# A diffusion transformer block on one core: bias products moved ahead of unit 0, their weights on the scalar queue, weight casts on GpSimd, and two units' statistics one beat later

## The chip, the cores and the metric

The kernel runs on 1 core of one Trainium2 chip. The metric is the device time of one execution in microseconds (us). The engines are TensorE (PE, matrix products; its weight loads are listed as PEld), VectorE (DVE), ScalarE (ACT), GpSimd (POOL) and SyncE (SP). SP issues most of the DMA transfers, ACT and POOL a few.

## The reference

A transformer block with adaptive layer norm, for 16 batch entries of 256 tokens with 256 channels, 16 heads of 16 channels, all in float32:

```python
shift_a, scale_a, gate_a, shift_m, scale_m, gate_m = split(silu(c) @ W_mod + b_mod, 6)
x_norm = ln(x) * (1 + scale_a) + shift_a
q, k, v = split(x_norm @ W_qkv + b_qkv, 3)
x = x + gate_a * (softmax(q k^T * hd**-0.5) v @ W_proj + b_proj)     # self attention
q_c = ln(x) @ W_qc + b_qc;  k_c, v_c = split(ln(context) @ W_kvc + b_kvc, 2)
x = x + (softmax(q_c k_c^T * hd**-0.5) v_c @ W_cproj + b_cproj)      # cross attention
x_norm2 = ln(x) * (1 + scale_m) + shift_m
x = x + gate_m * (gelu(x_norm2 @ W_mlp1 + b_mlp1) @ W_mlp2 + b_mlp2)
```

The biases of the values need not be added to the values: since attention weights sum to one, they can be carried through the projection. The kernel computes `gate_a`, `(bias_v @ W_proj + b_proj) * gate_a` and `bias_vc @ W_cproj + b_cproj` once, each as a narrow matrix product, and adds them later.

## The kernel before, in words

**Units and beats.** There are 32 attention units, numbered n = 0 to 31: self attention (`s`) of batch entries 0 to 3, then alternately self attention of entry b + 4 and cross attention (`c`) of entry b. The main loop runs `beat(n, k)` for n = -1 to 31 and k = 0 to 7. In beat (n, k), PE computes a first set of scores of unit n + 1 (tile `s`), whose row maxima VectorE takes (`mx`), and transposed scores of unit n (tile `st`), which ScalarE exponentiates (`pt`). In "unit -1", the slot ahead of unit 0, only the first scores of unit 0 are there. Between the scores stand the other units' pieces: layer norm statistics (`st_`, `mv_`, `rs_`, on VectorE), their power and application (`rs_`, `xn_`, on GpSimd), transposes (`psT_`), query, key and value products (`ps_q`, `ps_k`, `ps_v`, in "lanes" of two interleaved halves), the weighted sums (`o`), and the projection (`ps_P`). The scores use two PSUM banks, which the next scores may overwrite once `mx` has read them.

**High and low parts.** Products are made with a rounded high part and a low part of each operand (`h_`/`l_`, `xTh`/`xTl`, `W[0]`/`W[1]`). `split` makes the two parts of a weight: a copy that rounds, and a subtraction on GpSimd. Queries and keys are written to a stack (`big`) by DMA (`send`), with rows of ones (`one0`, `one1`, `one2`, for three buffers) and of negated maxima (`m`).

**Order.** Each engine keeps the program order of the code (`keep_in_program_order`). What stands outside the beats is placed by two tables of words: `PRE` is the order ahead of the loop, and `SL` says which words run at the end of which beat. `rest` takes one further step of the generator `setup_rest`. `cN` and `dN` are N products of zeros (`wz`), into a bank that is not in use. `ld2`, `ld3`, `ld4` load x of units 2, 3, 4. `HP` chooses the engine of the copy in `split`: 0 is VectorE, 1 is GpSimd; its first entry is for the weights of `setup_rest`.

**setup_rest before.** In ten steps: load `wga`, `wp` and the bias rows; load `wkc`, `wqc`; `ps_ga` and its sum into `gb`; `ps_pb`, two sums into `gb`, and the store `gd<-gb`; load `wvc`, `wcp`; split Wp, Wkc, Wqc, Wvc; `ps_cb`, its sum `bc`, the store `cd<-bc`, and the split of Wcp. All its DMAs are on SP. `gb` has a buffer of the tag `pt`, of which there are five.

**Statistics of self units.** In beat (n, 4) the statistics of unit n + 4 (`ls`) follow, on VectorE, those of the cross unit n + 3 (`lx`), where that unit's are taken in this beat (`late`: batch entries 0, 1, 14, 15). With a self unit at n + 4, this happens at n = 2 and n = 4.

Of the kernel before, what the change touches and what calls it, by code (L numbers as in the profile page):

```python
# [13 lines left out]
ALU = mybir.AluOpType  # L14
AX = mybir.AxisListType

P = 128
# [4 lines left out]
def pixart_block(  # L22
# [8 lines left out]
    B, N, H = x.shape  # L31
# [4 lines left out]
    KC = H // P  # L36
# [15 lines left out]
                return tc.keep_in_program_order(i) if self.on else i  # L52
            return issue

    E_ = {'M': ((-17, -12, -10, -1, 1), (0, 3, 4, 7, 9), (8, 11, 13, 15)), 'CUT': 8, 'LN': {'s': 'pool', 'c': 'pool', 'q': 'pool'}, 'ON': (1, 1, 1), 'L0': -16, 'L1': 1, 'S0': -7, 'A0': 0, 'T0': 1, 'H': (7, 11, 14, 15), 'S1': 5, 'A1': 7, 'L2': 9, 'T1': 9, 'S2': 32, 'AP': 23, 'DV': (0, 1), 'HP': (0, 0), 'BZ': {}, 'AV': {1: [(1, 2), (1, 3)], 9: [(0, 0), (0, 1)]}, 'AHEAD': (0, 0, 0, 0, 0, 2), 'W1P': [(-9, 1), (-8, 1), (-7, 1), (-6, 1), (-5, 1), (-5, 5), (-4, 1), (-4, 3), (-4, 5), (-3, 1), (-3, 3), (-3, 5), (-2, 1)], 'W2P': [(-4, 7), (-3, 0), (-3, 4), (-3, 6), (-3, 7), (-2, 2), (-2, 4), (-2, 6), (-1, 0), (-1, 1)], 'XP': 1, 'IL': 1, 'MF': 0, 'SH': 4, 'RAMP': 1, 'HA': 1, 'MP': 16, 'W': (7, 1, 0, 0), 'PRE': 'z0qp z0kp load silu b12 brow L0a turn L0b b4 L0d scale T0t sc1 hik lok T0h T0l b4 shift b4 hiq L1a L1b bk loq K0a K0b K0x0 K0x1 K0y0p K0y1p L1d T1t K0l T1h K0l0 K0l1 Q0a Q0m bq Q0h Q0x0 Q0y0p Q0x1 Q0y1p T1l Q0l Q0l0 Q0l1 z1kp z1qp K1a K1b hiv lov Q1a Q1b K1x0 K1x1 K1y0 K1y1 K1l K1l0 K1l1 ld2 Q1x0 Q1x1 Q1y0 Q1y1 Q1l Q1l0 Q1l1 V0a V0b bv b5 one0 vone ld3 z2kp z2qp', 'SL': {(-1, 0): 'one1 one2 c4', (-1, 1): 'ld4 L2a V1a', (-1, 2): 'L2b L2c V1b', (-1, 3): 'c5', (-1,4): 'M0 c4', (-1, 5): 'T2t T2h T2l c3', (-1, 6): 'rest L3a K2a c1', (-1, 7): 'K2m L3b L3p L3c c3', (0, 0): 'rest d4', (0, 1): 'rest', (0, 2): 'd3', (0, 3): 'rest', (0, 4): 'rest', (0, 5): 'rest', (0, 6): 'rest', (1, 1): 'rest', (1, 3): 'rest', (1, 5): 'rest', (30, 0): 'd3', (30, 1): 'd2', (30, 2): 'd3', (30, 5): 'd3', (31, 1): 'd2'}}

    PE = InOrder(nc.tensor, True)
    ACT, DVE, POOL, SP = (InOrder(e, True) for e in (nc.scalar, nc.vector, nc.gpsimd, nc.sync))
# [9 lines left out]
    def ps_gen(name, tag=None):  # L68


        if tag is None and ps_turn[0] is not None:
            ps_turn[0] ^= 1
            tag = (SHORT, LONG)[ps_turn[0]]
        tag = tag or SHORT
        return psum.tile([P, 512], F32, tag=tag, name=name, bufs=2)
# [16 lines left out]
    BMOD, BQKV, BQC, BKVC, BM1 = 0, 12, 18, 20, 24  # L92
# [11 lines left out]

    brow = const.tile([32, P], F32, name="brow")

    def stage(w_ap, c0, name, tag="pt", bufs=5, t=None):

        if t is None:
            t = work.tile([P, KC, H], F32, tag=tag, name=name, bufs=bufs)  # L110
        SP.dma_start(t, w_ap[:, c0:c0 + H].rearrange("(k p) c -> p k c", p=P))
        return t

    def split(hi, lo, src, eng=POOL, hp=0):
# [11 lines left out]
    sc1 = const.tile([P, 2, 2, B], F32, name="sc1")  # L126
    bT = const.tile([P, 32], F32, name="bT")
# [3 lines left out]
    cd = dram.tile([1, H], F32, name="cd", bufs=1)  # L131
# [89 lines left out]
    def setup_rest():  # L221
        gb = work.tile([B, 2, 2, H], F32, tag="pt", name="gb", bufs=5)
        gA, bb = gb[:, 0], gb[:, 1]
        bc = const.tile([1, H], F32, name="bc")
        wg, wp = stage(W_mod, 2 * H, "wga", "g", 3), stage(W_proj, 0, "wp_f", "g", 3)
        SP.dma_start(bb[:, 0], b_mod[2 * H:3 * H].partition_broadcast(B))
        SP.dma_start(bb[:, 1], b_proj.partition_broadcast(B))
        SP.dma_start(bc, b_cproj.partition_broadcast(1))
        yield
        wkc, wqc = stage(W_kvc, 0, "wkc_f", "g", 3), stage(W_qc, 0, "wqc_f", "c", 2)  # L230
        yield
        pst = ps_gen("ps_ga")
        for k in range(KC):
            PE.matmul(pst[:B, :H], sT[:, k], wg[:, k], start=(k == 0), stop=(k == KC - 1))
        DVE.tensor_tensor(gA[:, 0], pst[:B, :H], bb[:, 0], ALU.add)
        yield
        pst = ps_gen("ps_pb")
        for k in range(KC):
            PE.matmul(pst[:B, :H], bqkv[:, 4 + k], wp[:, k], start=(k == 0), stop=(k == KC - 1))
        DVE.tensor_tensor(gA[:, 1], pst[:B, :H], bb[:, 1], ALU.add)  # L240
        DVE.tensor_tensor(gA[:, 1], gA[:, 1], gA[:, 0], ALU.mult)
        SP.dma_start(gd[:, 0:2], gA)
        yield
        wvc, wcp = stage(W_kvc, H, "wvc_f", "x1", 5), stage(W_cproj, 0, "wcp_f", "x1", 5)
        yield
        split(Wp[0], Wp[1], wp)
        yield
        split(Wkc[0], Wkc[1], wkc)
        yield
        split(Wqc[0], Wqc[1], wqc)  # L250
        yield
        split(Wvc[0], Wvc[1], wvc)
        yield
        pst = ps_gen("ps_cb")
        for k in range(KC):
            PE.matmul(pst[:1, :H], bT[:, BKVC + 2 + k:BKVC + 3 + k], wcp[:, k],
                      start=(k == 0), stop=(k == KC - 1))
        DVE.tensor_tensor(bc, pst[:1, :H], bc, ALU.add)
        SP.dma_start(cd, bc)
        split(Wcp[0], Wcp[1], wcp)  # L260


# [423 lines left out]
    M = {}  # L686
# [256 lines left out]
    def beat(n, k):  # L943
# [29 lines left out]
        if k == 0:  # L973
            if cur:
                m_part(cur, 1)
            exps()
            if prev:
                av_part(prev, 2)
                av_part(prev, 3)
            if q2:  # L980
                q2.K.low()
                q2.K.send_low()
            if p3:
                p3.add()
            if ls and n > 0:
                load(ls)
            if lc:
                lc.ln[0].steps[0]()
            if p1:
                p1.gate()  # L990
        elif k == 1:
            exps()
            run(lanes(q2 and q2.Q, p2))
            if lc:
                lc.ln[0].steps[1]()
                lc.ln[0].steps[2]()
        elif k == 2:
            exps()
            if prev:
                p1.turn(1)  # L1000
            if q3T:
                q3T.T[0].turn()
                q3T.T[0].high()
            if p2 and p2.hurry:
                p2.add()
        elif k == 3:
            exps()
            if q3T and q3T.kind == "s":
                q3T.T[0].low()
            if prev:  # L1010
                p1.norm(1)
            run(lanes(q2 and q2.V, q2 and q2.Q))
            if q3T and q3T.kind == "c":
                q3T.T[0].low()
        elif k == 4:
            if nxt:
                m_part(nxt, 0)
            exps()
            if cur:
                av_part(cur, 0)  # L1020
                av_part(cur, 1)
            if prev:
                p1.aT.turn()
                p1.aT.high()
            if q2:
                q2.Q.low()
                q2.Q.send_low()
            if p3:
                p3.store()
            if late:  # L1030
                for f in lx.ln[1].steps:
                    f()
            if ls:
                ls.ln[0].steps[0]()
                ls.ln[0].steps[1](False)
        elif k == 5:
            exps()
            run(lanes(q3 and q3.K, q2 and q2.V))
            if prev:
                p1.aT.low()  # L1040
            if ls:
                ls.ln[0].pow()
                ls.ln[0].steps[2]()
            if early:
                early.ln[1].steps[0]()
            v = unit(n + 5)
            if v and v.kind == "c":
                load(v)
        elif k == 6:
            exps()  # L1050
            if cur:
                cur.post.begin()
                cur.post.turn(0)
            if lx:
                lx.T[1].turn()
                lx.T[1].high()
            if early:
                early.ln[1].steps[1]()
                early.ln[1].steps[2]()
            if prev and whole:  # L1060
                p1.proj(0)
                p1.proj(1)
        elif k == 7:
            exps()
            run(lanes(None if whole else p1, q3 and q3.K))
            if prev and whole:
                p1.end()
                p1.add()
                p1.store()
            if cur:  # L1070
                cur.post.norm(0)
            if lx:
                lx.T[1].low()
# [97 lines left out]
```

## Time and profile before

| | |
|---|---|
| Time, 3 runs | 819.60, 819.81, 820.62 us; median 819.81 |
| Profiled execution | 822.69 us, of which span 820.9 us |
| PE, PEld, DVE, ACT, POOL busy | 786.1, 662.8, 600.0, 584.6, 461.8 us |
| TensorE clock granted, mean | 0.997 of full speed |
| Costliest on VectorE: `mx` | 256 x 1223 ns |
| Costliest on ScalarE: `pt` | 256 x 1019 ns |
| HBM read, written | 26.97 MB, 8.46 MB |
| Chain that ended last | PE 66%, DVE 18%, issue 4%, POOL 3%, DMA 3% |

The span runs from the first to the last instruction; the time of an execution is longer by what lies around it. Busy time is the time in which an engine had an instruction under way. A row of a timeline gives the start in us, the duration in us, the engine, the line, the operation, output and inputs by the program's names, the shapes and types, how many instructions were merged, and in brackets the idle time before it and what ended it. Nearly all instructions carry the line of the recording helper (L51), so they are told apart by their tiles. "SPq" marks an issue by the queue of SP.

### The profile page before, as it was taken

To read this page: it belongs to the slowest core of one execution; us is meant where nothing else is said; L and a number is where in the kernel's file an instruction comes from. 1 tells how busy PE (TensorE), PEld (TensorE's weight loads), DVE (VectorE), ACT (ScalarE), POOL (GpSimd) and SP (SyncE) were. 2 spreads that over 40 slices of the span, in tenths; PEclk is the share of its full clock that TensorE was granted. 3 is DMA by queue.
4 is the path that set the end of the run, shared out by engine and by line. 5 is a ranking of instruction groups with operands and counts; after the bars stand their busy time and mean duration, and the time that the engine had idled before them with its cause. 6 is when DMAs were issued, how large, how long until landed. Compare 5 with 4: busy or idle time off the path is not lost.

```text
span 820.9 us, 23768 instructions
## 1 busy us (share of the span) xinstructions
PE 786.1 (96%) x9485; PEld 662.8 (81%) x9485; DVE 600.0 (73%) x1055; ACT 584.6 (71%) x1022; POOL 461.8 (56%) x399
## 2 busy tenths in 40 slices
PE   8899999999999999999999999999889999999997
PEld 8777777777787777778777778877658999999997
DVE  4787878888887888887787888777664566566562
ACT  3266878788887877878788888887556666665663
POOL 5544647464754636475463767654445656566663
PEclk9999999999999999999999999999999999999999
DMA  5553434344453444435344554534311212212211
GB/s 146 169 146 104 130 106 131 96 128 110 113 157 91 132 112 124 123 106 151 96 137 109 153 141 130 151 98 122 102 54 41 74 57 77 72 46 78 78 37 55
DMA packets 89938, 87.88 MB, mean 107 GB/s; under 512 B 9506, under 2 KB 85572, under 8 KB 89828
## 3 DMA queue, kind: packets, MB, share of 16 engines
q1 hardware_dynamic: 89364, 85.58, 37.0%
q8 instruction: 75, 1.23, 0.6%
q0 software_dynamic: 192, 0.52, 0.2%
q14 instruction: 35, 0.29, 0.1%
q10 hardware_dynamic: 272, 0.26, 0.1%
HBM read 26.97 MB, written 8.46 MB: 43 GB/s over the span
## 4 chain that ended last, share of the span: by engine, by line
PE 66%; DVE 18%; issue 4%; POOL 3%; DMA 3%; SPq 1%; ACT 1%; POOLq 0%; ACTq 0%
PE s L51 14%; DVE mx L51 12%; PE o L51 12%; PE ph L51 11%; PE st L51 9%; PE ps_q L51 3%; PE ps_kc L51 2%; PE ps_P_s L51 2%; PE ps_qc L51 2%; PE ps_k L51 2%; DMA c<-in_ctx_dram 2%; PE ps_v_s L51 1%; DVE xTl_s L51 1%; PE psT_m L51 1%; PE psm L51 1%
## 5 line engine op out<-in xcount | busy, mean ns | idle before, releaser
L51 DVE TENSOR_REDUCE mx<-s 128x4 f32<-128x1024 f32 x256 | 313.1, 1223 | 103.1 <-PE s L51 98.4
L51 ACT ACTIVATE pt<-st 128x1024 f32<-128x1024 f32 x256 | 260.9, 1019 | 54.6 <-PE st L51 45.4
L51 PE MATMUL s<-big 63*128 63x256 f32 x1024 | 121.2, 310 | 17.9 <-DVE mx L51 15.8
L51 PE MATMUL o<-pt,v 128*32 128x256 f32 x2048 | 123.8, 382 | 3.1 <-DVE A_s L51 3.1
L51 PEld LDWEIGHTS s<-big 63*128 63x128 f32 x1024 | 80.1, 186 | 55.4 <-DVE mx L51 34.3
L51 POOL TENSOR_TENSOR hl<-hf,hh 128x512 fp32r<-128x512 f32 x64 | 89.0, 1399 | 55.5 <-ACT hh L51 54.5
L51 PE MATMUL st<-big 64*128 64x256 f32 x1024 | 107.2, 282 | 2.3 <-ACT pt L51 2.3
L51 PEld LDWEIGHTS o<-pt,v 128*32 128x32 f32 x2048 | 60.0, 109 | 44.9 <-DVE A_s L51 5.7
L51 PEld LDWEIGHTS st<-big 64*128 64x128 f32 x1024 | 82.0, 188 | 4.4 <-ACT pt L51 2.9
L51 ACT ACTIVATE hf<-ph,bT 128x256 f32<-128x256 f32 x120 | 50.3, 473 | 28.1 <-PE ph L51 28.1
L51 ACT COPY oT<-o 128x512 f32<-128x512 f32 x63 | 36.9, 586 | 45.7 <-PE o L51 45.7
L51 ACT ACTIVATE hh<-ph,bT 128x256 fp32r<-128x256 f32 x120 | 50.4, 471 | 24.8 <-PE s L51 13.0
L51 POOL TENSOR_TENSOR xTl_as<-y_as,xTh_as 128x512 fp32r<-128x512 f32 x16 | 20.3, 1270 | 64.9 <-ACT y_as L51 64.9
L51 POOL TENSOR_TENSOR xTl_c<-y_c,xTh_c 128x512 fp32r<-128x512 f32 x16 | 20.6, 1290 | 61.7 <-PE s L51 52.9
L51 PE MATMUL ph<-wqch,wself 128*128 128x256 f32 x256 | 51.8, 285 | 0.0
L51 PE MATMUL ph<-wkch,wself 128*128 128x256 f32 x256 | 51.8, 286 | 0.0
L51 POOL TENSOR_TENSOR xTl_ac<-y_ac,xTh_ac 128x512 fp32r<-128x512 f32 x16 | 20.5, 1280 | 51.7 <-ACT y_ac L51 47.8
L51 PE MATMUL s<-big,hh 128*128 128x256 f32 x256 | 47.4, 282 | 0.0
L51 PE MATMUL st<-big,hh 128*128 128x256 f32 x256 | 47.2, 281 | 0.0
L51 DVE TENSOR_SCALAR xn_m<-x,mv_m,rs_m 128x256 f32<-128x256 f32 x32 | 38.3, 1236 | 10.8 <-POOL rs_m L51 10.8
L51 PEld LDWEIGHTS ph<-wqch,wself 128*128 128x128 f32 x256 | 42.0, 191 | 0.4 <-issue 0.4
L51 PEld LDWEIGHTS ph<-wkch,wself 128*128 128x128 f32 x256 | 41.9, 191 | 0.4
(221 smaller groups left out, 2381.9 us busy)
## 6 DMA issues: line engine op xcount, KB each, us to landing
big<-h_kc SPq DMA_DIRECT2D x64, 128.0 KB
big<-h_qc SPq DMA_DIRECT2D x64, 128.0 KB
big<-h_k SPq DMA_DIRECT2D x62, 128.0 KB
big<-h_q SPq DMA_DIRECT2D x62, 128.0 KB
big<-l_k SPq DMA_DIRECT2D x32, 128.0 KB
big<-l_q SPq DMA_DIRECT2D x32, 128.0 KB
c<-in_ctx_dram SPq DMA_DIRECT2D x16, 256.0 KB
g<-gd SPq DMA_DIRECT2D x16, 256.0 KB
```

The source lines that it names most:

```text
L51: i = f(*a, **k)
```

## The change

The three bias products (`ps_ga`, `ps_pb`, `ps_cb`) move to the beats 3, 4 and 5 of unit -1, where they stand in place of products of zeros (`c5`, `c4`, `c3`). Their weights (`wga`, `wp`, `wcp`) and bias rows are loaded together, by DMAs that the scalar queue issues, in the last part of `PRE`. The loads of `wkc`, `wqc` and `wvc` become one step, at the end of unit -1. The five splits follow in beats (0, 1), (0, 4), (1, 0), (1, 2), (1, 4), and their copies are on GpSimd. `ld2` moves ahead of the sends of unit 1; `one0`, `one1` and `one2` move from the end of `PRE` and beat (-1, 0) to the beats (-1, 0), (-1, 3) and (-1, 7). In the beats with `late`, all statistics of `ls` move from beat 4 to beat 5, behind that beat's `mx`.

```diff
-    E_ = {... 'HP': (0, 0), ...
+    E_ = {... 'HP': (1, 0), ...
 'PRE':
-  ... Q0l1 z1kp z1qp K1a ... K1l1 ld2 Q1x0 ... V0a V0b bv b5 one0 vone ld3 z2kp z2qp
+  ... Q0l1 ld2 z1kp z1qp K1a ... K1l1 Q1x0 ... V0a V0b bv b5 rest vone ld3 z2kp z2qp
 'SL':
-  (-1, 0): 'one1 one2 c4', (-1, 3): 'c5', (-1, 4): 'M0 c4', (-1, 5): 'T2t T2h T2l c3',
-  (-1, 6): 'rest L3a K2a c1', (-1, 7): 'K2m L3b L3p L3c c3', (0, 0): 'rest d4', (0, 1): 'rest',
-  (0, 2): 'd3', (0, 3): 'rest', (0, 4): 'rest', (0, 5): 'rest', (0, 6): 'rest',
-  (1, 1): 'rest', (1, 3): 'rest', (1, 5): 'rest'
+  (-1, 0): 'one0 c4', (-1, 3): 'rest one1', (-1, 4): 'M0 rest', (-1, 5): 'T2t T2h T2l rest',
+  (-1, 6): 'L3a K2a c1', (-1, 7): 'K2m L3b L3p L3c c3 one2 rest', (0, 0): 'd4', (0, 1): 'rest',
+  (0, 2): 'd3', (0, 4): 'rest', (1, 0): 'rest', (1, 2): 'rest', (1, 4): 'rest'
...
-    def stage(w_ap, c0, name, tag="pt", bufs=5, t=None):
+    def stage(w_ap, c0, name, tag="pt", bufs=5, t=None, q=SP):
...
-        SP.dma_start(t, w_ap[:, c0:c0 + H].rearrange("(k p) c -> p k c", p=P))
+        q.dma_start(t, w_ap[:, c0:c0 + H].rearrange("(k p) c -> p k c", p=P))
...
-        wg, wp = stage(W_mod, 2 * H, "wga", "g", 3), stage(W_proj, 0, "wp_f", "g", 3)
-        SP.dma_start(bb[:, 0], b_mod[2 * H:3 * H].partition_broadcast(B))
-        SP.dma_start(bb[:, 1], b_proj.partition_broadcast(B))
-        SP.dma_start(bc, b_cproj.partition_broadcast(1))
-        yield
-        wkc, wqc = stage(W_kvc, 0, "wkc_f", "g", 3), stage(W_qc, 0, "wqc_f", "c", 2)
+        wg, wp = stage(W_mod, 2 * H, "wga", "g", 3, q=ACT), stage(W_proj, 0, "wp_f", "g", 3, q=ACT)
+        ACT.dma_start(bb[:, 0], b_mod[2 * H:3 * H].partition_broadcast(B))
+        ACT.dma_start(bb[:, 1], b_proj.partition_broadcast(B))
+        ACT.dma_start(bc, b_cproj.partition_broadcast(1))
+        wcp = stage(W_cproj, 0, "wcp_f", "x1", 5, q=ACT)
...
-        wvc, wcp = stage(W_kvc, H, "wvc_f", "x1", 5), stage(W_cproj, 0, "wcp_f", "x1", 5)
...
         SP.dma_start(cd, bc)
+        yield
+        wkc, wqc = stage(W_kvc, 0, "wkc_f", "g", 3), stage(W_qc, 0, "wqc_f", "c", 2)
+        wvc = stage(W_kvc, H, "wvc_f", "x1", 5)
+        yield
+        split(Wp[0], Wp[1], wp)
...
-            if ls:
+            if ls and not late:
                 ls.ln[0].steps[0]()
                 ls.ln[0].steps[1](False)
         elif k == 5:
...
-            if ls:
+            if ls and late:
+                for f in ls.ln[0].steps:
+                    f()
+            elif ls:
                 ls.ln[0].pow()
                 ls.ln[0].steps[2]()
```

More of the change, by code (lines that the diff above doesn't have):

```diff
@@ L53, in __getattr__ @@
             return issue
-    E_ = {'M': ((-17, -12, -10, -1, 1), (0, 3, 4, 7, 9), (8, 11, 13, 15)), 'CUT': 8, 'LN': {'s': 'pool', 'c': 'pool', 'q': 'pool'}, 'ON': (1, 1, 1), 'L0': -16, 'L1': 1, 'S0': -7, 'A0': 0, 'T0': 1, 'H': (7, 11, 14, 15), 'S1': 5, 'A1': 7, 'L2': 9, 'T1': 9, 'S2': 32, 'AP': 23, 'DV': (0, 1), 'HP': (0, 0), 'BZ': {}, 'AV': {1: [(1, 2), (1, 3)], 9: [(0, 0), (0, 1)]}, 'AHEAD': (0, 0, 0, 0, 0, 2), 'W1P': [(-9, 1), (-8, 1), (-7, 1), (-6, 1), (-5, 1), (-5, 5), (-4, 1), (-4, 3), (-4, 5), (-3, 1), (-3, 3), (-3, 5), (-2, 1)], 'W2P': [(-4, 7), (-3, 0), (-3, 4), (-3, 6), (-3, 7), (-2, 2), (-2, 4), (-2, 6), (-1, 0), (-1, 1)], 'XP': 1, 'IL': 1, 'MF': 0, 'SH': 4, 'RAMP': 1, 'HA': 1, 'MP': 16, 'W': (7, 1, 0, 0), 'PRE': 'z0qp z0kp load silu b12 brow L0a turn L0b b4 L0d scale T0t sc1 hik lok T0h T0l b4 shift b4 hiq L1a L1b bk loq K0a K0b K0x0 K0x1 K0y0p K0y1p L1d T1t K0l T1h K0l0 K0l1 Q0a Q0m bq Q0h Q0x0 Q0y0p Q0x1 Q0y1p T1l Q0l Q0l0 Q0l1 z1kp z1qp K1a K1b hiv lov Q1a Q1b K1x0 K1x1 K1y0 K1y1 K1l K1l0 K1l1 ld2 Q1x0 Q1x1 Q1y0 Q1y1 Q1l Q1l0 Q1l1 V0a V0b bv b5 one0 vone ld3 z2kp z2qp', 'SL': {(-1, 0): 'one1 one2 c4', (-1, 1): 'ld4 L2a V1a', (-1, 2): 'L2b L2c V1b', (-1, 3): 'c5', (-1,4): 'M0 c4', (-1, 5): 'T2t T2h T2l c3', (-1, 6): 'rest L3a K2a c1', (-1, 7): 'K2m L3b L3p L3c c3', (0, 0): 'rest d4', (0, 1): 'rest', (0, 2): 'd3', (0, 3): 'rest', (0, 4): 'rest', (0, 5): 'rest', (0, 6): 'rest', (1, 1): 'rest', (1, 3): 'rest', (1, 5): 'rest', (30, 0): 'd3', (30, 1): 'd2', (30, 2): 'd3', (30, 5): 'd3', (31, 1): 'd2'}}
@@ new lines, in pixart_block @@
+    E_ = {'M': ((-17, -12, -10, -1, 1), (0, 3, 4, 7, 9), (8, 11, 13, 15)), 'CUT': 8, 'LN': {'s': 'pool', 'c': 'pool', 'q': 'pool'}, 'ON': (1, 1, 1), 'L0': -16, 'L1': 1, 'S0': -7, 'A0': 0, 'T0': 1, 'H': (7, 11, 14, 15), 'S1': 5, 'A1': 7, 'L2': 9, 'T1': 9, 'S2': 32, 'AP': 23, 'DV': (0, 1), 'HP': (1, 0), 'BZ': {}, 'AV': {1: [(1, 2), (1, 3)], 9: [(0, 0), (0, 1)]}, 'AHEAD': (0, 0, 0, 0, 0, 2), 'W1P': [(-9, 1), (-8, 1), (-7, 1), (-6, 1), (-5, 1), (-5, 5), (-4, 1), (-4, 3), (-4, 5), (-3, 1), (-3, 3), (-3, 5), (-2, 1)], 'W2P': [(-4, 7), (-3, 0), (-3, 4), (-3, 6), (-3, 7), (-2, 2), (-2, 4), (-2, 6), (-1, 0), (-1, 1)], 'XP': 1, 'IL': 1, 'MF': 0, 'SH': 4, 'RAMP': 1, 'HA': 1, 'MP': 16, 'W': (7, 1, 0, 0), 'PRE': 'z0qp z0kp load silu b12 brow L0a turn L0b b4 L0d scale T0t sc1 hik lok T0h T0l b4 shift b4 hiq L1a L1b bk loq K0a K0b K0x0 K0x1 K0y0p K0y1p L1d T1t K0l T1h K0l0 K0l1 Q0a Q0m bq Q0h Q0x0 Q0y0p Q0x1 Q0y1p T1l Q0l Q0l0 Q0l1 ld2 z1kp z1qp K1a K1b hiv lov Q1a Q1b K1x0 K1x1 K1y0 K1y1 K1l K1l0 K1l1 Q1x0 Q1x1 Q1y0 Q1y1 Q1l Q1l0 Q1l1 V0a V0b bv b5 rest vone ld3 z2kp z2qp', 'SL': {(-1, 0): 'one0 c4', (-1, 1): 'ld4 L2a V1a', (-1, 2): 'L2b L2c V1b', (-1, 3): 'rest one1', (-1,4): 'M0 rest', (-1, 5): 'T2t T2h T2l rest', (-1, 6): 'L3a K2a c1', (-1, 7): 'K2m L3b L3p L3c c3 one2 rest', (0, 0): 'd4', (0, 1): 'rest', (0, 2): 'd3', (0, 4): 'rest', (1, 0): 'rest', (1, 2): 'rest', (1, 4): 'rest', (30, 0): 'd3', (30, 1): 'd2', (30, 2): 'd3', (30, 5): 'd3', (31, 1): 'd2'}}
@@ L243, in setup_rest @@
         yield
-        wvc, wcp = stage(W_kvc, H, "wvc_f", "x1", 5), stage(W_cproj, 0, "wcp_f", "x1", 5)
+        pst = ps_gen("ps_cb")
+        for k in range(KC):
+            PE.matmul(pst[:1, :H], bT[:, BKVC + 2 + k:BKVC + 3 + k], wcp[:, k],
+                      start=(k == 0), stop=(k == KC - 1))
+        DVE.tensor_tensor(bc, pst[:1, :H], bc, ALU.add)
+        SP.dma_start(cd, bc)
+        yield
+        wkc, wqc = stage(W_kvc, 0, "wkc_f", "g", 3), stage(W_qc, 0, "wqc_f", "c", 2)
+        wvc = stage(W_kvc, H, "wvc_f", "x1", 5)
         yield
@@ L253, in setup_rest @@
         yield
[L254 to L259, printed above, removed]
         split(Wcp[0], Wcp[1], wcp)
```

## The prediction

> **What bounds the kernel now.** I read the busy shares first, then stretches by unit, then VectorE row by row from 25 to 82 us, where the edits lie, and last the granted clock.
>
> ```profile
> span 820.9 us, 23768 instructions
> PE 786.1 (96%) x9485; PEld 662.8 (81%) x9485; DVE 600.0 (73%) x1055; ACT 584.6 (71%) x1022; POOL 461.8 (56%) x399
> ```
>
> TensorE is nearly always busy and VectorE's `mx` is next: a beat is scores (`s`), then their row maximum (`mx`), which frees the banks for the next scores. From `mx` to `mx` a beat with no extras takes 1.82 us. The stretches run from the first `mx` of one unit's beats to the next: units -1, 0, 1, 2, 3.
>
> ```profile
> 25.66:40.85 15.19, 13.43 (x105) 10.90 (x105) 12.44 (x20) 2.53 (x6) 5.46 (x6) 1.00 0.51 152
> 40.85:60.22 19.37, 18.37 (x204) 14.21 (x200) 15.41 (x27) 11.48 (x17) 8.51 (x8) 1.00 0.49 135
> 60.22:81.88 21.66, 19.78 (x237) 15.16 (x234) 15.57 (x27) 13.53 (x22) 10.36 (x10) 0.92 0.41 115
> 81.88:99.90 18.02, 17.52 (x250) 14.03 (x246) 14.53 (x26) 14.94 (x25) 11.08 (x10) 1.00 0.48 133
> 99.90:117.72 17.82, 16.97 (x246) 13.55 (x242) 14.22 (x24) 14.01 (x23) 10.56 (x10) 1.00 0.38 107
> ```
>
> Columns: stretch, length, busy us of PE, weight loads, VectorE, ScalarE, GpSimd, granted clock, DMA. Unit 1 does less than unit 3, yet is 3.84 us longer and alone has a clock below 1. Its VectorE rows, and unit 0's, name the causes:
>
> ```profile
> 48.99 0.87 DVE L51 SCALAR_TENSOR_TENSOR xTl_s<-psT_s,sc,xTh_s 128x256 fp32r<-128x256 f32 x2
> 50.48 0.41 DVE L51 TENSOR_TENSOR gb<-ps_pb,gb 16x256 f32<-16x256 f32 x1 [0.62 <-PE ps_pb L51]
> 50.92 0.41 DVE L51 TENSOR_TENSOR gb<-gb 16x256 f32<-16x256 f32 x1
> 51.27 1.21 DVE L51 TENSOR_REDUCE mx<-s 128x4 f32<-128x1024 f32 x1
> ...
> 61.36 0.87 DVE L51 SCALAR_TENSOR_TENSOR l_k<-ps_k,bqkv,h_k 128x256 fp32r<-128x256 f32 x2
> 63.50 0.75 DVE L51 BATCH_NORM_STATS2 st_c<-c 128x6 f32<-128x256 f32 x2 [1.27 <-DMA c<-in_ctx_dram]
> 64.17 1.21 DVE L51 TENSOR_REDUCE mx<-s 128x4 f32<-128x1024 f32 x1
> ```
>
> `mx` stands behind the bias sums, and behind statistics of a context tile that lands late. After that wait the clock halves:
>
> ```profile
> 62.07:65.48 3.41, 2.56 (x30) 2.00 (x22) 2.14 (x6) 1.61 (x2) 1.08 (x1) 1.00 0.65 190
> 65.48:68.89 3.41, 3.41 (x22) 2.85 (x24) 1.76 (x4) 1.54 (x3) 3.16 (x4) 0.53 0.29 78
> ```
>
> **The change, part by part.** Terms are shifts of the `mx` chain, in the time of the profiled execution (822.69 us, span 820.9). It is 2.88 above the median 819.81; I take the same saving off both.
>
> *Unit -1, added: +0.4.* `ps_ga` (0.97 on PE) takes the place of five zero products (1.38), `ps_pb` of four (1.06), `ps_cb` of three (0.83). PE still ends each before `mx` frees the banks, save `ps_cb`: 34.68 + 0.58 of transposes + 0.97 = 36.2, under VectorE's 36.24. On VectorE, which idles 0.60 ahead of `mx`, the first `gb` sum (0.41) hides. The next two (0.79 to the next `mx`) delay one `mx` by 0.2, absorbed because `xTl` waits for ScalarE's `xTh` until 36.21 anyway. `bc` (0.41) follows `xTl` directly and is paid. Bounds: 0.34 (overlap of VectorE rows) to 1.64 (all four exposed).
>
> *Unit 0, removed.* `ps_ga` at 44.41 stands between the lanes and the next scores, whose banks were free at 44.0: -0.97. `ps_pb` and two sums: scores could end at 49.9 and `xTl` ends at 49.86, so `mx` at 51.27 moves to 49.95: -1.32. Next, `pt` waits 1.38 for `gd<-gb` to free its buffer, holding PE's `st` 0.51. With that gone, PE reaches the scores of beat 6 at 53.3 on this scale and `mx` stands at 53.8 where it was 56.34, 2.55 earlier: -0.26 more. The casts of `wself` and `wkch` (0.42) lie before `mx` rows that wait for PE by 0.55 and 0.27: nothing.
>
> *Unit 1, removed.* `c` is issued at 58.45, behind two weight loads and a queue that had stood at `gd`, and lands 5.03 later. In the new order the sends follow at once and the loads are out of its way: sync issues it near 54.8, `st_c` is due near 60.0, so 5.2 suffice; unit 3's `st_c` at 101.83, of a `c` issued at 96.67, waits for nothing. -1.2. With no wait PE idles at most 0.3, and I take the half clock as gone: beat 2 to 3 took 3.06 against 1.82 in unit 3: -1.24 (bounds 0 to -1.71, half of 3.41). `wqch` hides; `wvch` delays `mx` by 0.33, but the `o` products wait for `A_s` as before: nothing net. `ps_cb`, `bc` and `wcph` make beat 5 to 6 3.35 long against 1.92: -1.43. Check: 21.66 - 3.87 = 17.79, beside unit 3's 17.82.
>
> *GpSimd's five copies: nothing, if short.* The trace has no GpSimd copy. Bounds: 0.54 (memset of 128x512) to 2.44 (two 128x256 scalar operations); I take 1.28, the subtraction of the same shape. Three copies and three subtractions (7.7) stand ahead of `xTl_as`, with `xg`, `rs_c` and `xn_c` (1.3 + 0.8 + 2.4). Starting when `g` lands, 58.7 to 61.1, they end by 70.7 to 73.4; with `xTl_as`, 72.0 to 74.7. PE needs it at 80.96 - 5.9 = 75.05.
>
> The Trainium skill speaks against this move: "GPSIMD Engine Reference", Engine selection, says not to put elementwise work there, two-input operations being about twice as slow, one-input roughly at line rate. The trace agrees on the first: VectorE casts in 0.42, GpSimd subtracts in 1.28. By the page's 1.03 cycles an element a copy would be about 0.44 plus dispatch (an estimate), and the sum unchanged.
>
> *Self statistics (units 2 and 4): -0.2.* Three kinds of rows (1.0 to 1.1 in all) leave the space before `mx` at 94.36, whose scores were done at 93.55: `mx` 0.76 earlier. They then stand before the next one: 0.41 earlier. Then PE's `psT_q` waits for `xn_q`, which GpSimd ends at 96.68 either way: 0.1 remains, twice. Bounds 0 to -1.5.
>
> *Queues.* The scalar queue stands idle from 23.81 to 30.22; six issues of 0.28 to 0.61 fit. But the new order lets `bc` wait for `wga` and `wcp` for `wp` to land, and ScalarE's `v` copy (due 30.22, used by `psm` at 32.85) stands behind them; sync's third `h_q` send waits for `gb`. `ld2` fills a wait of sync's. `one0`, `one1`, `one2` pass x loads and are needed from 40.7 on. `wkc`, `wqc`, `wvc` now stand before unit 2's `h_k` sends: 0.8 late, needed a unit later; `m` follows them to about 45.2, due at 49.2.
>
> **Sum:** +0.4 - 0.97 - 1.32 - 0.26 - 1.2 - 1.24 - 1.43 - 0.2 = -6.2. Profiled 816.5, median 813.6. Later units repeat their own beats, so the lead is kept.
>
> **The rivals.**
>
> *Slow GpSimd copies.* At 2.44 each, three add 3.5 to a margin of 0.3 to 3.0: PE stands 0.5 to 3.2 at `xTl_as`; the middle, 1.8, gives 815.4. For: two-scalar operations take 1.22 for half the elements. Against: a copy reads one operand less than the 1.28 row.
>
> *The half clock stays, or comes into unit -1*, where narrow products (16 columns, 1 column) take over from full zeros: 814.8 for one stretch, 816.5 if a new one costs 1.7 on top. For: it came in a window where PE was busy 2.56 of 3.41. Against: 27.93 to 31.35 had 2.60 and stayed full. The skill's "TensorE: Matmul & The Clock Gate", on the idle window, says half rate follows at least one idle window of about 3.4 us. The trace's stretch is 3.41 long, as it says, but PE had idled only 0.85 before it, so the row decides; by the page alone, removing that wait need not bring the clock back, and the sum would be -5.0.
>
> *The scalar queue lands late: slower.* PE stands in order at `ps_cb`, due 35.3. At the slowest landing in these rows (5.03), `wp`, issued at 24.4, lands at 29.4, and `wcp` after it at 34.5 to 35.0: just in time. Each microsecond beyond is paid in full; from `wcp` at 41.5 the gain is gone. At 10 us a landing it comes at 44.4: 9.1 lost, 2.9 slower, 822.7. For: q1 sends share the engines, busy 0.79 from 24.5 to 27.9. Against: 0.60 and 0.34 after that.
>
> **How the numbers follow.** Forecast 0.62; copies 0.12; clock 0.14; late landings 0.12, of which 0.08 beyond the whole gain and 0.04 near it. A measurement of this kernel tells about 0.2% (1.6 us) from no change, so faster 0.88, same 0.04, slower 0.08. The range goes down by the rest of the statistics' bound (1.3) and part of the +0.4 to 812.0, and up to 817.2 over the copies and both clock cases; the late landings stay out.
>
> **What would show it.** Right: stretches near 15.6, 16.8 and 17.8 for units -1, 0 and 1; `st_c` and `pt` without DMA waits; clock 1.00 throughout; GpSimd copies under 1.5. Wrong: PE waiting for `wga`, `wp` or `wcp`; a half-clock stretch; `xTl_as` ending after its lane begins. The forecast falls if units 0 and 1 together save under 4 us.

## The result, and the profile after

The changed kernel takes 815.53 us (median of 6 runs, 815.27 to 815.80) against 819.75 us for the kernel before in the same comparison (6 runs, 819.09 to 824.08): a ratio of 0.994, 95% interval 0.9919 to 0.9960. It is faster, by 0.6%, and the time lies inside the forecast's range (812.0 to 817.2), but the saving of the medians is 4.2 us where 6.2 was forecast. The two profiled executions differ by more, 822.69 to 815.38, which is 7.3. Most of the study is about these two distances from 6.2.

The page of the changed kernel, and its stretches by unit (-1 to 3) with the columns of the stretches shown before:

```profile
span 813.6 us, 23717 instructions
PE 780.9 (96%) x9461; PEld 658.9 (81%) x9461; DVE 597.9 (73%) x1050; ACT 585.2 (72%) x1022; POOL 464.6 (57%) x404
```

```profile
25.55:41.07 15.52, 13.23 (x93) 8.90 (x93) 13.76 (x25) 2.53 (x6) 5.47 (x6) 1.00 0.61 167
41.07:57.35 16.28, 15.78 (x196) 13.43 (x192) 13.50 (x21) 11.38 (x17) 9.64 (x10) 1.00 0.54 157
57.35:75.24 17.89, 16.93 (x234) 13.52 (x230) 14.61 (x23) 13.45 (x22) 11.47 (x12) 1.00 0.43 116
75.24:93.04 17.80, 17.40 (x250) 13.96 (x246) 14.68 (x27) 14.93 (x25) 10.93 (x10) 1.00 0.46 128
93.04:111.03 17.99, 17.12 (x246) 13.73 (x242) 14.21 (x23) 14.17 (x24) 10.93 (x10) 1.00 0.39 108
```

Units -1, 0 and 1 take 15.52, 16.28 and 17.89 (forecast 15.6, 16.8, 17.8) where they took 15.19, 19.37 and 21.66, together 6.53 less. Unit 1 costs no more than its neighbours, and the clock is 1.00 in every stretch.

VectorE's rows of the changed kernel show the sums in unit -1, and unit 1 without its wait:

```profile
34.03 0.41 DVE L51 TENSOR_TENSOR gb<-ps_pb,gb 16x256 f32<-16x256 f32 x1
34.47 0.41 DVE L51 TENSOR_TENSOR gb<-gb 16x256 f32<-16x256 f32 x1
34.82 1.21 DVE L51 TENSOR_REDUCE mx<-s 128x4 f32<-128x1024 f32 x1
36.13 0.88 DVE L51 SCALAR_TENSOR_TENSOR xTl_s<-psT_s,sc,xTh_s 128x256 fp32r<-128x256 f32 x2
36.93 0.40 DVE L51 TENSOR_TENSOR bc<-ps_cb,bc 1x256 f32<-1x256 f32 x1
37.26 1.20 DVE L51 TENSOR_REDUCE mx<-s 128x4 f32<-128x1024 f32 x1
...
58.49 0.87 DVE L51 SCALAR_TENSOR_TENSOR l_k<-ps_k,bqkv,h_k 128x256 fp32r<-128x256 f32 x2
59.28 0.74 DVE L51 BATCH_NORM_STATS2 st_c<-c 128x6 f32<-128x256 f32 x2
60.10 1.23 DVE L51 TENSOR_REDUCE mx<-s 128x4 f32<-128x1024 f32 x1
```

The last `mx` shown of unit -1 stands directly behind `bc`, as the forecast had it; unit -1 is the only one of the three that is longer, by 0.33. In unit 1 `st_c` follows `l_k` without a gap, so the context tile is there in time.

GpSimd's rows show the copies, and the scalar queue's rows the early loads:

```profile
65.47 0.61 POOL L51 CAST wvch<-wvc_f 128x512 fp32r<-128x512 f32 x1
66.17 1.29 POOL L51 TENSOR_TENSOR wvcl<-wvc_f,wvch 128x512 fp32r<-128x512 f32 x1
67.39 0.62 POOL L51 CAST wcph<-wcp_f 128x512 fp32r<-128x512 f32 x1
68.08 1.27 POOL L51 TENSOR_TENSOR wcpl<-wcp_f,wcph 128x512 fp32r<-128x512 f32 x1
71.47 1.27 POOL L51 TENSOR_TENSOR xTl_as<-y_as,xTh_as 128x512 fp32r<-128x512 f32 x1 [2.12 <-ACT y_as L51]
```

```profile
27.19 0.46 ACTq L51 DMA_DIRECT2D bc<-in_L_xcond_b_cproj_dram  x1
28.25 0.40 ACTq L51 DMA_DIRECT2D wcp_f<-in_L_xcond_W_cproj_dram  x1
30.11 0.59 ACT L51 COPY v<-psv_s 128x512 f32<-128x512 f32 x1 [6.41 <-PE psv_s L51]
```

A copy takes 0.61 to 0.62 us, half of the 1.28 that the forecast took, and `xTl_as` starts after GpSimd has been idle for 2.12: TensorE doesn't wait for the copies. The scalar queue's last two issues come late (the four before them went out from 23.11 to 25.28), but ScalarE's `v` copy is on time, and TensorE waits for none of the three early weights.

### The profile page after: what moved, and what is told of

Read it like the earlier page. It is cut to its first block, busy times and chain, and to the rows that moved or that the text cites. A ratio compares the mean times of both kernels' runs of the same rounds, so it can differ in the third digit from the quotient of the medians.

```text
span 813.6 us, 23717 instructions
## 1 busy us (share of the span) xinstructions
PE 780.9 (96%) x9461; PEld 658.9 (81%) x9461; DVE 597.9 (73%) x1050; ACT 585.2 (72%) x1022; POOL 464.6 (57%) x404
## 4 chain that ended last, share of the span: by engine, by line
PE 69%; DVE 16%; issue 5%; POOL 4%; DMA 1%; ACT 0%; SPq 0%; POOLq 0%
PE s L51 15%; PE o L51 13%; DVE mx L51 12%; PE ph L51 11%; PE st L51 9%; PE ps_q L51 3%; PE ps_kc L51 3%; PE ps_k L51 3%; PE ps_P_s L51 2%; PE ps_qc L51 2%; PE ps_v_s L51 1%; PE ps_P_c L51 1%; DVE xTl_s L51 1%; PE psm L51 1%; PE psT_m L51 1%
```

## The experiments

The theory (A in most expectations): the terms of the sum hold in every execution, save that the half clock of unit 1 and some late landings belong to single executions, so that a profiled pair and the medians differ. The rival: the terms were too large, and part of what was removed had been hidden. The runs were made in three groups, each on one chip together with the kernel before, and the ratio is to that; the medians of the kernel before in the three are 820.09, 820.51 and 820.23. "The changed kernel" below is 815.42, the median of its 12 executions in two comparisons, and 76 executions of the kernel before (64 as the partner in three comparisons, 12 of the first experiment) have the median 820.42.

**The kernel before, once more.** No edit.

> The kernel before, profiled once more and timed against itself; ratio 1.000. Theory A (the two single executions that were profiled differ by more than the kernels do): the half-clock stretch of unit 1 and part of the late landings belong to that one execution, so this profile has a span nearer to 818 than to 820.9, and where the stretch is missing, the distance from the third to the fourth row maximum of unit 1 is about 1.8 us in place of 3.06. Theory B (the terms of the sum are too large by 2 us): the half-clock stretch is there again at the same place, the span is 820 to 821, and the shortfall of the medians lies in other terms.

Measured: 821.25 (818.84 to 824.13, 12 runs), ratio 1.0015 (1.0002 to 1.0028); the profiled execution has a span of 818.2. Its page, VectorE in unit 1, and two stretches of 3.41 us, the one that holds the wait and the one after it:

```profile
span 818.2 us, 23768 instructions
```

```profile
64.40 0.75 DVE L51 BATCH_NORM_STATS2 st_c<-c 128x6 f32<-128x256 f32 x2 [1.44 <-DMA c<-in_ctx_dram]
65.07 1.21 DVE L51 TENSOR_REDUCE mx<-s 128x4 f32<-128x1024 f32 x1
...
66.88 1.22 DVE L51 TENSOR_REDUCE mx<-s 128x4 f32<-128x1024 f32 x1
68.70 1.23 DVE L51 TENSOR_REDUCE mx<-s 128x4 f32<-128x1024 f32 x1 [0.60 <-PE s L51]
```

```profile
62.97:66.38 3.41, 2.40 (x30) 2.02 (x22) 1.98 (x5) 1.61 (x2) 1.04 (x1) 1.00 0.58 172
66.38:69.79 3.41, 3.35 (x42) 2.98 (x44) 2.78 (x5) 2.60 (x4) 3.20 (x4) 1.00 0.28 77
```

The wait for the context tile is there again, even longer (1.44 against 1.27), and TensorE was less busy in the stretch around it (2.40 of 3.41 against 2.56), yet the clock stays at 1.00 and the beat after takes 1.82. So the same program with the same wait is met by the half clock in one execution and not in another. Theory A holds on that. How often it is met can be read from the mean clock of each execution: 20 of the 76 have 0.997 or less, with a median of 822.17; the other 56 have 819.96. No execution of the changed kernel is under 0.998. (A mean doesn't say where a half-clock stretch lies. One stretch of 3.41 at half takes about 0.2% off it, two take 0.4%; ten of the thirteen profiles also have up to 3 us at half clock at the very end, behind TensorE's last product, which cost no time and take up to 0.2% off.)

The span differs from the first profile's by 2.68 in all. Counted from `mx` to `mx`, 1.24 is the clock, and about 2.1 are two steps of 1.0 and 1.1 at the beats that open units 13 and 15, which this profile lacks. It starts its first `mx` 0.67 later.

The ratio says something on the method, too: the same program against itself came out 1.2 us slower in the median, with an interval that does not reach 1. Distances of about 1 us between medians, here and below, are not told from nothing.

**Statistics back at their place.**

```diff
-            if ls and not late:
+            if ls:
                 ls.ln[0].steps[0]()
                 ls.ln[0].steps[1](False)
 ...
-            if ls and late:
-                for f in ls.ln[0].steps:
-                    f()
-            elif ls:
+            if ls:
                 ls.ln[0].pow()
```

> The changed kernel with the self statistics of units 2 and 4 back at their old place. Theory A (terms as forecast): 0.2 us slower than the changed kernel, about 815.7, beat 5 of units 2 and 4 0.76 later and beat 6 no more than 0.2 later. Theory B (the move costs more than it gives, since the statistics stand before the next row maximum): 0.3 to 1.0 us faster than the changed kernel, about 815.0.

Measured: 815.03 (814.06 to 815.64, 6 runs), ratio 0.9935 (0.9921 to 0.9949). VectorE in unit 2, first of the changed kernel, then of this one:

```profile
86.95 1.23 DVE L51 TENSOR_REDUCE mx<-s 128x4 f32<-128x1024 f32 x1 [0.24 <-PE s L51]
88.10 0.74 DVE L51 BATCH_NORM_STATS2 st_s<-x 128x6 f32<-128x256 f32 x2
...
89.31 1.21 DVE L51 TENSOR_REDUCE mx<-s 128x4 f32<-128x1024 f32 x1
```

```profile
87.25 0.75 DVE L51 BATCH_NORM_STATS2 st_s<-x 128x6 f32<-128x256 f32 x2
...
88.35 1.21 DVE L51 TENSOR_REDUCE mx<-s 128x4 f32<-128x1024 f32 x1
90.16 1.22 DVE L51 TENSOR_REDUCE mx<-s 128x4 f32<-128x1024 f32 x1 [0.60 <-PE s L51]
```

The distance between the two `mx` goes from 2.36 to 1.81 when the statistics stand ahead of both, after a first one that is later by 0.77 on the scale of the units: of the 0.77 the move gives back 0.55. The 0.22 remain, twice (units 2 and 4). In unit 5 the move loses 0.24, from the second `mx` to the third: there VectorE's `rs_c` takes 1.21, where it takes 0.98 with the statistics back and 0.17 at its shortest. In the changed kernel:

```profile
132.99 1.21 DVE L51 TENSOR_SCALAR rs_c<-mv_c 128x2 f32<-128x2 f32 x1
```

```profile
132.89 1.29 POOL L51 TENSOR_TENSOR x<-xg,t_s 128x512 f32<-128x512 f32 x1
```

`rs_c` ends 0.02 after GpSimd's `x`, and so it does in this run (134.87 and 134.85): an earlier beat only makes it longer. No run here shows what couples the two. The changed kernel's first profile loses another 0.18 at the beat that opens unit 4, its second doesn't. Units 2 to 5 together take 72.05 here and 71.85 in the changed kernel's second profile, so by the traces the move is worth 0.2, theory A's size. The median, 0.4 under the changed kernel and within B's range, can't tell: that kernel's own two comparisons lie as far apart (815.53 and 815.06).

**Casts back on VectorE.**

```diff
-    'HP': (1, 0)
+    'HP': (0, 0)
```

> The changed kernel with the five weight casts on VectorE. Theory A (casts stand partly before row maxima): five casts of 0.42 us are 2.1 us at most; two of them meet beats where the row maximum waits for TensorE, so 0.4 to 1.2 us slower than the changed kernel, 815.9 to 816.7. Theory B (the casts were hidden on VectorE before, too, and the move to GpSimd is worth nothing): within 0.3 us of the changed kernel, 815.3 to 815.8.

Measured: 814.99 (814.66 to 816.03, 6 runs), ratio 0.9937 (0.9924 to 0.9950): nearer to theory B, 0.3 under its range, and nothing of A in the median. In the trace one row maximum is later for good, by 0.33 in beat (0, 5), behind the cast of `wkch`; the one behind `wqch` is 0.16 later and the next beat gives it back, and the other casts leave no step.

**Products back in units 0 and 1**, with the early loads, their queue, the casts and the statistics left as in the changed kernel.

```diff
 # SL
-  (-1, 3): 'rest one1', (-1, 4): 'M0 rest', (-1, 5): 'T2t T2h T2l rest'
+  (-1, 3): 'one1 c5', (-1, 4): 'M0 c4', (-1, 5): 'T2t T2h T2l c3'
-  (0, 1): 'rest', (0, 2): 'd3', (0, 4): 'rest', ... (1, 4): 'rest'
+  (0, 1): 'rest rest', (0, 2): 'd3', (0, 3): 'rest', (0, 4): 'rest', ... (1, 4): 'rest', (1, 5): 'rest'
 # setup_rest: the steps stand in the order: early loads; later loads (with ps_ga);
 # ps_pb; splits; ps_cb
```

> The changed kernel's loads, queues, casts and statistics, but the zero products back in the slot ahead of unit 0, and the bias products and their sums back in units 0 and 1. Theory A (the terms of the sum hold in every execution): loses 0.97 + 1.32 + 0.26 + 1.43 and gets the 0.33 of unit -1 back, so 3.65 us slower than the changed kernel, 819.2; the context tile of unit 1 still lands in time and the clock stays at 1.00. Theory B (the products and sums were half hidden, and the medians' shortfall of 2 us lies there): 1.6 us slower, 817.1.

Measured: 819.21 (817.59 to 821.31, 12 runs), ratio 0.9990 (0.9978 to 1.0001). Its stretches of units -1, 0 and 1:

```profile
26.27:41.46 15.19, 13.42 (x105) 10.86 (x105) 12.43 (x21) 2.53 (x6) 5.45 (x6) 1.00 0.57 155
41.46:60.69 19.23, 18.21 (x204) 14.17 (x200) 14.74 (x24) 11.44 (x17) 9.63 (x10) 1.00 0.52 139
60.69:79.84 19.15, 18.09 (x238) 13.82 (x234) 15.12 (x25) 13.55 (x22) 11.25 (x12) 1.00 0.41 114
```

3.85 us more than the changed kernel in these three (53.57 against 49.72, the mean of its two profiles), and 3.79 in the medians, where 3.65 was expected. Theory B is out: the products and sums are worth their full terms here, in the profile and in the medians. (The beat of `bc` is 1.16 longer and not 1.43, since the cast of `wcph` is on GpSimd in this run; `ps_ga` and `ps_pb` are 0.2 longer each.) It is also the split of the whole: the products are three quarters of the saving that the large samples show (5.0), and the relief of the queue, though the wait for the context tile is gone here, brings 0.9 of 820.09 beside it (its interval reaches to none).

One part of A did not hold: 2 of the 12 executions have a clock of 0.997. In the profiled one the tile is in time and the clock is full, so a half clock is not tied to this wait alone; where those two have theirs was not profiled.

**The changed kernel once more.** No edit.

> The changed kernel once more, as the yardstick for the runs beside it. Theory A (a landing of the low query parts decides, in odd units from 9 on, whether one beat is 1.1 us longer, and which units are hit differs by execution): the median lies within 0.6 us of 815.5, and the profile shows the 1.1 us step in other units than unit 19, or in none. Theory B (the step belongs to the program): unit 19 is hit again.

Measured: 815.06 (814.54 to 816.42, 6 runs), ratio 0.9930 (0.9912 to 0.9947). Units -1 to 1 repeat to 0.07 us (49.76 against 49.69), and the step of 1.1 at unit 19 is gone; there is none at another unit. Theory B is out: the step belongs to an execution. That it comes from a landing, as A has it, is not shown by this.

**A fill where TensorE waits for the context tile.** To the kernel before:

```diff
-  (1, 1): 'rest'
+  (1, 1): 'rest d3'
```

> The kernel before with three zero products (0.83 us on TensorE) put in unit 1's second beat, where TensorE idles 0.85 us for the context tile; nothing else is changed. Theory A (the half-clock stretch follows that idle time, and only in some executions): no run has a granted clock under 0.998, the slow tail above 821 us is gone, and the median moves by 0 to -0.6 us, since most executions had no such stretch. Theory B (the idle time has nothing to do with it): about every third run still has a clock of 0.995 to 0.997 and takes over 821 us.

Measured: 820.45 (819.83 to 822.70, 12 runs), ratio 1.0002 (0.9990 to 1.0014). All 12 executions have a clock of 0.998 or more, where 4 of 24 of the kernel before beside it have 0.997 or less. Around the wait TensorE is now busy throughout:

```profile
61.80:65.21 3.41, 3.41 (x46) 2.61 (x36) 2.87 (x8) 2.14 (x3) 1.00 (x1) 1.00 0.74 225
65.21:68.62 3.41, 3.35 (x38) 2.86 (x39) 2.25 (x5) 1.92 (x4) 3.20 (x4) 1.00 0.31 85
```

```profile
63.22 0.75 DVE L51 BATCH_NORM_STATS2 st_c<-c 128x6 f32<-128x256 f32 x2 [0.54 <-DMA c<-in_ctx_dram]
```

In this execution the tile came earlier than in the other two profiles (a wait of 0.54, not 1.27 or 1.44), so the profile alone says little about the fill; the twelve clocks have to.

Theory A on the clock, though 12 executions alone could miss a stretch that one in four has about once in thirty times (0.74 to the twelfth power is 0.03). The part of A that failed is the tail: 5 of the 12 take over 821 us at full clock; the profiled one, 822.09, has two steps of 1.1, at units 13 and 17. The median doesn't move, as is to be expected where most executions lack the stretch.

**The gate sums' store on GpSimd's queue.** To the kernel before:

```diff
-        SP.dma_start(gd[:, 0:2], gA)
+        POOL.dma_start(gd[:, 0:2], gA)
```

> The kernel before with the one store of the gate sums issued by GpSimd's queue, so that sync doesn't stand at it. Theory A (sync's queue is what makes the context tile of unit 1 late): its statistics wait for no transfer, the row maximum behind them comes 1.2 us earlier, the half-clock stretch is gone, and the median is 1.2 to 1.6 us lower than the kernel before, 818.5 to 818.9. Theory B (the two weight loads ahead of it share the transfer engines, and these make it late): the wait stays at 0.8 us or more, and the median moves by less than 0.5.

Measured: 821.29 (819.55 to 822.30, 12 runs), ratio 1.0002 (0.9991 to 1.0014). VectorE's row for the context tile, ScalarE's in unit 0, and the store among the issues (the last number is us from issue to landing):

```profile
62.83 0.74 DVE L51 BATCH_NORM_STATS2 st_c<-c 128x6 f32<-128x256 f32 x2
```

```profile
53.60 1.02 ACT L51 ACTIVATE pt<-st 128x1024 f32<-128x1024 f32 x1 [2.39 <-DVE mv_s L51]
```

```profile
gd<-gb POOLq DMA_DIRECT2D x1, 32.0 KB, 2.4
```

Sync no longer stands at the store, the context tile is issued at 56.24 (58.45 before) and its statistics wait for nothing, though both weight loads still stand ahead of it. So far theory A is right. But sync's stand at the store is only half of the cause. In the run with the products back sync still issues the store behind the sums (at 51.99), and the weight loads alone are out of the way. Sync's rows for the tile, first of the kernel before, then of that run:

```profile
58.45 0.47 SPq L51 DMA_DIRECT2D c<-in_ctx_dram  x1
```

```profile
58.33 0.58 SPq L51 DMA_DIRECT2D c<-in_ctx_dram  x1
```

Counted from the first `mx` (25.66 and 26.27) it is issued only 0.7 earlier there, yet it has landed by 4.3 after its issue, when `st_c` starts without a wait, where it took 5.03 before. In these two runs taking away either the stand at the store or the loads is enough.

The clock is at 0.999 or more in all 12 executions; with the fill that makes 24 without a half clock in mid-kernel that a mean would show, where a quarter would be 6, and the share of the 24 beside them 4. But nothing is saved, since another wait pays for it: `pt` needs the buffer that the store reads, and waits 2.39 where it waited 1.38; the beats after it are 1.1 later. The store was issued at 51.18 and landed 2.4 later, and `pt` starts at 53.60. The profile names `mv_s`, which ended at about the same time; but `pt` doesn't read it, and in the kernel before the same `pt` waits for the store by name. In the kernel before this one small store holds both the queue and the buffer, and moving its products out of unit 0 frees both at once.

**The early loads on sync.** To the changed kernel:

```diff
-        wg, wp = stage(W_mod, 2 * H, "wga", "g", 3, q=ACT), stage(W_proj, 0, "wp_f", "g", 3, q=ACT)
-        ACT.dma_start(bb[:, 0], ...)   # and bb[:, 1], bc, wcp
+        wg, wp = stage(W_mod, 2 * H, "wga", "g", 3), stage(W_proj, 0, "wp_f", "g", 3)
+        SP.dma_start(bb[:, 0], ...)    # and bb[:, 1], bc, wcp
```

> The changed kernel with its six early loads issued by sync in place of ScalarE. Theory A (it is the early place in the order and not the queue that counts): the six issues delay the sends of unit 0's keys by some 2.7 us, which are needed only at 40, and the time is within 0.4 us of the changed kernel. Theory B (the scalar queue is needed, since sync's sends of unit 0 and the loads are in each other's way): TensorE waits for a key or query part near 40 or for a weight near 31 to 35, and the time is 1 to 3 us longer, 816.5 to 818.5.

Measured: 815.76 (815.23 to 819.80, 7 runs), ratio 0.9946 (0.9926 to 0.9966). Sync issues the six from 29.07 to 31.97, behind the sends of queries, and TensorE waits for the first:

```profile
PE ps_ga L51 <- DMA wga<-in_L_xcond_W_mod_dram: 0.9, 1, 0.9
```

The beat is 0.55 longer, the other two weights are in time, and the median is 0.3 above the changed kernel: nearer to A than to B. Two of the 7 executions have a clock of 0.997 and 0.995 and take 817.78 and 819.80, so the wait in unit -1 may bring the half clock back in some of them; where those stretches lie was not profiled.

**Low query sends on GpSimd's queue, or on the scalar queue.** To the changed kernel, for the steps of 1.1 at odd units:

```diff
                 q2.Q.low()
-                q2.Q.send_low()
+                [q2.Q.send(f, 2, POOL) for f in range(KC)]     # or ACT
```

> The changed kernel with the two sends of the low query parts, from unit 2 on, issued by GpSimd's queue in place of sync's, where they stood behind the four high sends and the two of the row maxima (in unit 19 of the changed kernel's first profile they were ready at 369.15 and issued at 373.10). Theory A (the spread of the executions comes from scores that wait for these sends, because sync issues them late): no beat that opens an odd unit is 1.1 us longer, the spread narrows to under 1 us, and the median falls by 0.5 to 1.2 us, to 814.0 to 814.7. Theory B (the transfers themselves are late, whichever queue issues them, or GpSimd's issues take its time from its other work): no narrower, or 0.5 to 3 us slower.

> The same two sends on the scalar queue. Theory A: the 1.1 us steps are gone here, too, but ScalarE spends two issues of 0.3 to 0.6 us in each unit ahead of an exponential, so at best 0.5 us faster than the changed kernel, and up to 10 us slower if these issues stand ahead of work that TensorE waits for. Theory B (the landing itself is late): the steps stay, with that cost on top.

Measured on GpSimd's queue: 817.06 (816.42 to 817.67, 12 runs), ratio 0.9961 (0.9948 to 0.9975). The sends of unit 19, issued at 373.10 in the changed kernel, go out as soon as they are ready:

```profile
370.99 1.13 POOL L51 DMA_DIRECT2D big<-l_q  x2 [0.92 <-DVE l_q L51]
```

No step of 1.1 is in its profile, and 12 executions lie within 1.25 us of each other (12 of the changed kernel: 1.88; 76 of before: 5.99). That doesn't show theory A's mechanism: three of the profiles with these sends on sync's queue (the changed kernel once more, the early loads on sync, both parts undone) have no such step either, and the spread is not under 1. In time the run is theory B's, 1.6 slower: many units are some 0.08 longer, and from the first `mx` to the last it takes 1.9 us more than the changed kernel's second profile, more than the steps were worth. On the scalar queue it is 827.97 (826.35 to 829.30, 6 runs), ratio 1.0095 (1.0073 to 1.0116): 0.3 to 0.5 in most units, 12.5 in all, which is more than the 10 that were expected at worst. Neither beats the changed kernel, and what makes the steps of 1.1 stays open.

**Casts and statistics both undone.** The diffs of the second and third experiment together.

> The changed kernel without its two lesser parts: casts on VectorE and the self statistics at their old place; the early loads and the products in the slot ahead of unit 0 stay. Theory A (by the medians of the two single runs, which were 815.0 each, both parts are worth nothing that shows): 814.7 to 815.5, no more than 0.3 from the changed kernel. Theory B (each covers for the other, by the terms 0.2 for the statistics and 0.33 for the cast that showed in the first run's trace): 0.5 slower, 815.8.

Measured: 815.62 (814.96 to 816.01, 6 runs), ratio 0.9944 (0.9923 to 0.9965): between the theories, 0.1 over A's upper end and 0.2 under B's number, and 0.2 from the changed kernel. The profile has B's terms: against the changed kernel's second one it is 0.3 longer in units -1 to 1 (50.06) and 0.16 in units 2 to 5 (72.00). The two lesser parts of the change are worth about 0.5 by the traces, and nothing that a median of six shows, alone or together.

## Why the prediction was right, and where it was off

All profiles but that of the scalar queue, from the start of `mx` to the start of `mx` (us; "u -1 to 1" is the sum of the three stretches):

| profiled execution | u -1 to 1 | u 2 to 5 | u 6 to 28 |
|---|---|---|---|
| before | 56.22 | 72.05 | 409.02 |
| before, once more | 55.13 | 72.07 | 406.78 |
| products back | 53.57 | 71.86 | 409.43 |
| fill | 54.90 | 72.07 | 409.35 |
| store on GpSimd's queue | 54.97 | 72.21 | 409.09 |
| changed | 49.69 | 72.02 | 408.52 |
| changed, once more | 49.76 | 71.85 | 408.03 |
| statistics back | 49.71 | 72.05 | 407.87 |
| casts back | 50.02 | 71.84 | 407.73 |
| both undone | 50.06 | 72.00 | 407.67 |
| early loads on sync | 50.14 | 71.99 | 407.38 |
| low query sends on GpSimd's queue | 49.77 | 72.40 | 409.20 |

The first column is steady and is where the change acts. The last spreads by 2.7 us among kernels that are alike there (all but the last row).

**Right: the terms of units -1 to 1.** By the sum they should give 6.02 with the half clock and 4.78 without. They give 6.53 and 5.4 (56.22 and 55.13 less 49.7). Term by term, from the first pair of profiles:

- Unit -1 cost 0.33 (forecast 0.4), all of it around `bc`.
- `ps_ga` gave 1.15 (0.97), `ps_pb` with its sums 1.49 (1.32), and `pt` without its wait 0.28 (0.26).
- The context tile gave 1.20 (1.2), and the half clock 1.25 (1.24). Not forecast: the beat ahead of the tile is 0.17 shorter, which stays unexplained, and the beat behind it 0.11 longer, since VectorE's `rs_c` takes 0.67 in place of 0.17 there; it ends at 62.18, GpSimd's subtraction for `wqcl` at 62.15.
- `ps_cb`, `bc` and the cast gave 1.44 (1.43); `wvch` moved 0.33 and gave it back, as worked out.

That later units keep the lead holds, too, within the spread of the last column.

**The step that failed: "I take the same saving off both."** The saving was summed against one execution, 822.69, and taken off a median, 819.81. But that execution had the half clock of unit 1. By the mean clock about one execution in four has a half-clock stretch at all, so that most of the 1.24 is not in a median: 6.2 less 1.24 is 4.96. The three runs that stood for before were low besides: 819.81, where 76 executions give 820.42. Together 1.24 and 0.61 are 1.85 of the 1.9 that the forecast was too low. From the larger samples, 820.42 - 4.96 = 815.46 beside 815.42; so close a fit is partly chance, since the last column moves each execution by up to 2.7. The profiles' 5.4 off the 819.96 of executions at full clock would give 814.6. What the other 0.8 is stays open; it is less than the 1.2 between two medians of one and the same program. The steps at odd units don't explain it: they were rather rarer in the profiles with the products moved (3 in six, against 8 in the five others), which would add to the saving.

The forecast's rival "the half clock stays" put one stretch at 1.24 on top, 814.8, and so came nearer to the median for another reason: the clock did not stay in the changed kernel, it had mostly been absent before. The skill's "TensorE: Matmul & The Clock Gate", Part 1, says that the gate watches a free-running window of about 3.4 us, and that the number of slow products at a kernel's start therefore differs from run to run. The runs here agree as far as they go: the stretch was 3.41 long, and the same wait halved the clock in one profile and not in the next. On what brings it they differ from the page's full idle window: TensorE was busy for 2.56 us of the 3.41 before it.

**Mis-sized without effect: the copy on GpSimd.** Taken at 1.28 from the subtraction, it took 0.62. "GPSIMD Engine Reference", Engine selection, has GpSimd about twice as slow as VectorE in two-input operations and roughly at line rate in one-input ones. The prediction set VectorE's cast beside GpSimd's subtraction; the fair pair is VectorE's own subtraction of this shape, from the kernel before:

```profile
20.86 0.69 DVE L51 TENSOR_TENSOR wself<-wf,wself 128x512 fp32r<-128x512 f32 x1 [1.73 <-ACT wself L51]
```

GpSimd's 1.28 is 1.9 times that, as the page says. In the one-input copy it is 0.62 against 0.41 to 0.47, about 1.4 times. Since TensorE doesn't wait for the copies, the sum doesn't change. Nor, by the third experiment, does the median tell on which engine the copies are. (The prediction's end of GpSimd's work, 70.7, is 58.7 and 12.2, which make 70.9; nothing hangs on it.)

**The statistics, -0.2: right in size, by another path, and so partly by luck.** The forecast had 0.1 left in each of units 2 and 4. In each 0.22 is left, and 0.24 is lost in unit 5, where `rs_c` ends with GpSimd's sum. The forecast followed the move to its own unit's end and not to the next. In the table, units 2 to 5 take 71.84 to 72.02 with the move (the last row apart) and 72.00 to 72.21 without it.

**Late landings on the scalar queue** did not come: the two held-up issues went out at 27.19 and 28.25, and the products were not late. On sync the first load did come late, by 0.9 at the product and 0.55 in the beat, so the price that this rival put in full for each microsecond was too high there.

## What to carry to other kernels

Before a saving that is read in one profile is taken off a median, profile the kernel twice: a stall that only one execution has (here 1.24 us of half clock, and steps of 1.1 us) is no saving in the median. Moving narrow products and their small sums out of a full pipeline into its filling stage was worth 3.8 us, their whole length, because there they took the place of products of zeros and of idle time of VectorE. Before moving one transfer to another queue, list who waits for its end: the store that no longer held sync held the exponential's buffer 1.0 us longer, and the median stayed.

## What the runs showed of the hardware that was not expected

- The half clock after a wait is a matter of the execution: TensorE busy 2.56 of 3.41 us led to it once, 2.40 of 3.41 did not.
- GpSimd casts 128x512 from f32 to fp32r in 0.60 to 0.62 us, VectorE in 0.41 to 0.47, while GpSimd's subtraction for the same weights takes 1.27 to 1.31 and VectorE's 0.69.
- A VectorE row of two columns, `rs_c`, takes 0.17 us in four of its 16 calls in the changed kernel. In the other twelve it takes 0.28 to 1.21 and ends 0.02 to 0.03 after a two-input operation of GpSimd that was under way when it began.
- Of six loads issued in a row by the scalar queue, the fifth went out 1.9 us after the fourth had been issued; sync issued the same six from 29.07 to 31.97 without such a gap. The cause of the gap is not shown.
- Two issues per unit on GpSimd's queue (1.13 us for the pair) lengthen many units by some 0.08, on ScalarE's most by 0.3 to 0.5.
